# Two scattered rows per node, summed at the end, or one row per node to which the scatters add

## The chip, the cores and the metric

The kernel runs on one core of one Trainium2 chip. The metric is the time that the device takes for one launch, in microseconds (us). Before the change it is 1894.54 us, the median of three runs (1893.64 to 1895.57).

A core has five engines that work side by side, each on its own ordered list of instructions. TensorE (PE in the profile) does matrix products and has a separate step that loads weights (PEld). VectorE (DVE) and ScalarE (ACT) do elementwise work and sums. GpSimd (POOL) does some elementwise work and issues the indirect transfers: gathers and scatters of rows whose numbers are read from a list. SyncE (SP) issues most of the plain transfers. The transfers (DMA) move data between the large memory (HBM) and the on-chip memory (SBUF). Products are gathered in a small memory of their own, PSUM. An engine that needs the result of another, or of a transfer, waits for a semaphore; everything behind that instruction on the same engine waits too.

## The reference, cut to what matters

There are 3125 nodes with 256 features and 100,000 edges. The layer is

```python
xn = layernorm(x)
x  = x + gnn(xn, edge_attr_3, src, dst) + mixer(xn)     # mixer: 4 layers of linear attention and FFN
x  = x + ffn(layernorm(x))
```

The last line is a mixture of 16 experts, and the change touches only that part. For each node `y = layernorm(x)`:

```python
logits     = y @ gate_w + gate_b              # 16 numbers
vals, idx  = top_k(logits, 2)                 # the node's two experts
w          = softmax(vals)                    # two gates
e_k        = relu(y @ w1[idx_k] + b1[idx_k]) @ w2[idx_k] + b2[idx_k]    # 256 -> 512 -> 256
z          = y + w_0 * e_0 + w_1 * e_1
ffn(y)     = layernorm(z) * gamma + beta
```

So two experts' outputs of each node have to be added, with `y`, before the last normalisation. A sum over the 256 features of `z` cannot start before both are there.

## The kernel before, in words

**Tiling.** The nodes lie as 125 partitions by 25 tiles (`TP` = 125, `NT` = 25): partition p holds nodes 25p to 25p+24. `xm`, the running result, stays in SBUF for the whole kernel. The edge part and the first three mixer layers take the first 1600 us or so, and the change does not touch them.

**Dispatch, inside the last mixer layer.** The last mixer layer runs over seven blocks of nodes, the ranges in `BLOCKS`. Behind each block follow `stage_yn`, which normalises the block and stores *half* of `y` to the table `ynodes` in HBM; `stage_logits`, which picks the two experts and gates; and `stage_ranks`, which gives each (node, expert) pair a slot: expert e owns the slots that follow e * `CAP`. For each pair a record of three words (node, row of `outs` to write, gate) is scattered to the table `slots` in HBM. `prepare`, called in block 0 of that layer, clears what must be clear beforehand: it sets the rows of `ynodes` that are not yet written to zero, and fills `slots` with records of unused slots, each of which names a row of its own behind the real ones. Its stores go on SP's queue, where `slots`, and after them the loads `xr` and `xnT` of the next blocks, stand behind.

**The table `outs`.** It has two rows per node and one row per slot: `K * N + NSL` rows of 256 numbers. The first choice of node n goes to row n, the second to row N + n, and unused slots write rows that nobody reads. So no two slots write the same row.

**Expert tiles.** A tile is one expert and 128 or 256 of its slots, in blocks of 128. For each tile SP loads `ids` (128 records a block) and `ew` (the expert's weights, 1154 KB); POOL gathers the nodes of each block from `ynodes` into `yg` (L140); PE transposes them (`stage_t`), multiplies with `w1` (`stage_e1`), and with `w2` (`stage_e2`). DVE adds `b2` and then forms gate * expert + half of y in `o` (L209), and POOL scatters the 128 rows of `o` to `outs` (L211). The two halves of y that a node's two slots bring make the whole y.

- Four full tiles of two blocks are worked inside the first phase, behind the last mixer block ("early" tiles). They use memory that is free by then: `mem_h`, that is `hNT`, holds their weights, `mem_q`, that is `qT`, their `yg`, `hs` and `o`.
- The other tiles are worked by `run_tiles` in the second phase: 16 of one block and 17 of two blocks, mostly by turns. It loads `ids` six tiles ahead (nine buffers), weights and nodes three ahead (four buffers of `ew`, six of `yg`); `o` has three buffers. On PE and ACT the order is that of the program text. The line `stage_e2(xs[i - 1], 1)`, with tile i-1's last scatter, stands behind the load of the nodes of tile i+3, and so POOL's queue alternates between gathers and scatters.
- Two branches (`tc.If`) follow for more tiles than that; with these inputs nothing is in them to do.

**What orders the scatters.** The planner that places semaphores would make two writes to one table wait for each other. Here each scatter is put in a group, "combine", whose members are declared free of each other:

```python
tc.declare_no_dep(i.ins, group="combine", reason="every slot has a row of its own")
tc.add_to_no_dep_group("combine", i.ins)
```

So a scatter waits only for its `o`. What waits for a scatter's landing is the next user of its buffers (`ids`, `o`), and the output stage.

**Output stage.** It goes in ten parts of the 25 tiles (`ends`). SP loads both rows of each node into `ogs` (125 x 2 x 25 x 256), in 40 transfers, since `by_parts` cuts each into 112 and 13 partitions. PE adds the two rows by two products with the identity into PSUM (`sum_ps`, L1429). DVE takes mean and variance from there (`stats`: L91, L92), for the last tile of the larger parts ACT does (`act_stats`); ACT takes the root, DVE the reciprocal (L1452), ACT normalises from PSUM into `ogs` (L1456), DVE multiplies by `gamma` (L1461) and adds `xm` (L1462), which has `beta` in it already, and the part is stored.

**Memory.** `ogs`, `gamma` and an unused tile called `room` lie at the start of the second phase's memory; the weights' buffers `ew` and the tiles' working buffers follow. Nothing there is used before the first phase has left the addresses below it, and the planner adds the waits for that.

Of the kernel before, what the change touches and what calls it, by code (L numbers as in the profile page):

```python
# [16 lines left out]
N = 3125  # L17
# [24 lines left out]
K = 2  # L42
# [23 lines left out]
def gps_layer(ctx: ExitStack, tc: tile.TileContext, a, out):  # L66
# [10 lines left out]
    def by_tile(rows):  # L77

        return rows.rearrange("(p t) d -> p t d", t=NT)
# [20 lines left out]
    ynodes = tables.tile([N, D], F32, name="ynodes")  # L100
    slots = tables.tile([NSL, 3], I32, name="slots")

    outs = tables.tile([K * N + NSL, D], F32, name="outs")

    rs_v = consts.tile([TP, NT], F32, name="rs_v")
    rs_u = consts.tile([TP, NT], F32, name="rs_u")
# [24 lines left out]
    def registers(to, ap, most):  # L131
        to.extend(nc.values_load_multi_w_load_instructions(
            ap, engines=SP, min_val=0, max_val=most,
            skip_runtime_bounds_check_because="its parts are cut off above")[1])

    def expert_stages(new, mm_tile, fm_tile):
        def load_nodes(x):
# [54 lines left out]
        def stage_e2(x, part):  # L192
            n, ids = x["n"], x["ids"]
            if part == 0:
                x["e2"] = mm_tile("e2_ps").rearrange("p (j d) -> p j d", d=D)
                x["o"] = new("o")
            ps, o = x["e2"], x["o"]
            fs = range(NEF)
            if n == 1:
                fs = range(part * NEF // 2, (part + 1) * NEF // 2)  # L200
            j = part if n == 2 else 0

            for f in fs:
                nc.tensor.matmul(ps[:, j, :], x["hs"][:, f, j * P:(j + 1) * P], x["w2"][:, f, :],
                                 start=(f == 0), stop=(f == NEF - 1))
            if fs[-1] < NEF - 1:
                return
            nc.vector.tensor_add(o[:, j, :], ps[:, j, :], x["b2"])
            nc.vector.scalar_tensor_tensor(o[:, j, :], o[:, j, :], ids.bitcast(F32)[:, j, 2:3],  # L209
                                           x["yg"][:, j, :], op0=ALU.mult, op1=ALU.add)  # L210
            i = nc.gpsimd.indirect_dma_start(  # L211
                out=outs, out_offset=bass.IndirectOffsetOnAxis(ap=ids[:, j, 1:2], axis=0),
                in_=o[:, j, :], in_offset=None)
            tc.declare_no_dep(i.ins, group="combine", reason="every slot has a row of its own")
            tc.add_to_no_dep_group("combine", i.ins)

        return load_nodes, load_weights, stage_t, stage_e1, stage_ht, stage_e2

# [1 line left out]
    with ExitStack() as ph:  # L220
# [835 lines left out]

        def prepare():
            nc.gpsimd.memset(none, 0.0)
            for r in BLOCKS[-3:]:
                by_parts(nc.sync, by_tile(ynodes)[:, r[0]:r[-1] + 1, :], none[:, :len(r), :])  # L1060
            nc.gpsimd.memset(unused, 0)
            nc.gpsimd.iota(unused[:, :, 1], pattern=[[1, NSL // P]], base=K * N, channel_multiplier=NSL // P)
            nc.sync.dma_start(slots.rearrange("(p j) c -> p j c", p=P), unused)
            for k in range(K):
                nc.gpsimd.iota(rec[:, :, k, 0], pattern=[[1, NT]], base=0, channel_multiplier=NT)
                nc.gpsimd.iota(rec[:, :, k, 1], pattern=[[1, NT]], base=k * N, channel_multiplier=NT)
            nc.gpsimd.iota(eid, pattern=[[1, E]], base=0, channel_multiplier=0,
                           allow_small_or_imprecise_dtypes=True)
            nc.vector.memset(earlier, 1.0)
            nc.gpsimd.affine_select(out=earlier, in_=earlier, compare_op=ALU.is_gt, fill=0.0, base=0,  # L1070
                                    pattern=[[1, TP]], channel_multiplier=-1)
            nc.vector.memset(every, 1.0)
            nc.vector.tensor_scalar(run[:, 0, :], eid, float(CAP), None, op0=ALU.mult)
            nc.gpsimd.iota(tid, pattern=[[1, NFX]], base=0, channel_multiplier=0,
                           allow_small_or_imprecise_dtypes=True)
            nc.gpsimd.iota(spare, pattern=[[ST, NFX + NFE]], base=E * CAP, channel_multiplier=0,
                           allow_small_or_imprecise_dtypes=True)
            nc.vector.memset(one, 1.0)
            nc.vector.tensor_scalar(slot0, eid[:1], float(CAP), None, op0=ALU.mult)
# [243 lines left out]
    with ExitStack() as ph:  # L1323
# [6 lines left out]
        def mm_tile(name):  # L1330
            return psum.tile([P, 512], F32, tag="mm", name=name)

        ogs = big.tile([TP, K, NT, D], F32, name="ogs")
        gamma = big.tile([P, D], F32, name="gamma")

        big.tile([P, 2304], F32, name="room")
# [77 lines left out]
        ends = [1, 3, 5, 8, 11, 15, 19, 22, 24, NT]  # L1414
        parts = [range(i, j) for i, j in zip([0] + ends, ends)]
        for r in parts:
            for k in range(K):
                by_parts(nc.sync, ogs[:, k, r[0]:r[-1] + 1, :],
                         by_tile(outs[k * N:(k + 1) * N, :])[:, r[0]:r[-1] + 1, :])
        pss = {}  # L1420

        def sums(r):
            for q in groups(len(r), 2):
                t0, m = r[q[0]], len(q)
                pool, tag = ((psum, "mm"), (ps_f, "fm"))[q[0] // 2]
                ps = pool.tile([P, 512], F32, tag=tag, name="sum_ps")[:TP, :m * D].rearrange(
                    "p (i d) -> p i d", d=D)
                for k in range(K):
                    nc.tensor.matmul(ps, ident[:TP, :TP], ogs[:, k, t0:t0 + m, :],  # L1429
                                     start=(k == 0), stop=(k == K - 1))  # L1430
                for i in range(m):
                    pss[t0 + i] = ps[:, i, :]
                    if len(r) < 3 or t0 + i < r[-1]:
                        stats(tmp, ps[:, i, :], t0 + i)
                    else:
                        act_stats(ps[:, i, :], t0 + i)

        def act_stats(src, t):
            sq = tmp.tile([TP, D], F32, name="sq")
# [10 lines left out]
        def normalized(r, tt):  # L1450
            nr = tmp.tile([TP, 4], F32, name="nr")
            nc.vector.reciprocal(rstd[:, tt], rs_v[:, tt])  # L1452
            nc.vector.scalar_tensor_tensor(nr[:, :len(r)], mv[:, tt, 0], -1.0, rstd[:, tt], op0=ALU.mult,  # L1453
                                           op1=ALU.mult)
            for i, t in enumerate(r):
                nc.scalar.activation(ogs[:, 0, t, :], pss[t], AF.Identity, scale=rstd[:, t:t + 1],  # L1456
                                     bias=nr[:, i:i + 1])

        def stored(r, tt):
            ys = ogs[:, 0, tt, :]  # L1460
            nc.vector.tensor_mul(ys, ys, gamma[:TP, None, :].to_broadcast([TP, len(r), D]))  # L1461
            nc.vector.tensor_add(ys, ys, xm[:, tt, :])  # L1462

            by_parts(nc.gpsimd if r[0] < 15 else nc.sync, ov[:, tt, :], ys)

        with tc.manual_schedule(engines={mybir.EngineType.PE, mybir.EngineType.Activation, mybir.EngineType.DVE}):
            last = None
            for r in parts:
                sums(r)
                tt = scales(r)  # L1470
                if last:
                    stored(*last)
                normalized(r, tt)
                last = r, tt
            stored(*last)
# [61 lines left out]
```

## Time and profile before

| what | where from | value |
|---|---|---|
| time of a launch | median of three runs | 1894.54 us |
| profiled execution | one run with the profiler | 2133.78 us, span 2132.1 us, mean granted clock 0.934 |
| last mixer layer's first part, 1600 to 1680 us | table by stage | PE busy 80.00 of 80, clock 1.00, DMA 0.20 |
| rest of it with the early tiles, 1680 to 1880 us | table by stage | PE busy 190.92 of 200, clock 0.98, DMA 0.26 |
| expert tiles, 1890 to 2048 us | table by stage | PE busy 156.64 of 158, clock 1.00, DMA 0.79 |
| last tiles and branches, 2048 to 2086 us | table by stage | PE busy 27.32 of 38, clock 0.90, DMA 0.29 |
| output stage, 2086 to 2132 us | table by stage | PE busy 25.20, DVE 29.74, ACT 21.09 of 46, clock 0.83, DMA 0.68 |

The profile records one execution, and this one took longer than the runs that make up the median; a duration from the profile belongs to the profiled execution. The page gives for each engine its busy time, its share of the span and the number of its instructions. A table by stage has for each stretch of time (from:to, in us) its length, then busy time and number of instructions of each engine, the mean clock that was granted to PE, the mean share of the DMA engines that was busy, and what they moved in GB/s. A row of an engine's order of time has the start and the duration in us, the engine, the line, what was written and read, and in brackets how long the engine had been idle before and what ended that ("issue" is time in which it waited for nothing that the profile shows). SPq is the queue of transfers that SP issues: its rows show how long SP stood at the issue.

### The profile page before, as it was taken

Reading aid. Unit: us, or ns where it says so; the run is one execution under the profiler, and the core shown is the slowest. Engines: PE = TensorE matmul, PEld = TensorE weight load, DVE = VectorE, ACT = ScalarE, POOL = GpSimd, SP = SyncE. Lnnn points to the kernel's source line nnn. Section 1 sums busy time; section 2 is a strip of 40 time slices with the busy share of each in tenths; the row PEclk is TensorE's granted clock in tenths of the full one; section 3 lists DMA queues with packets and bytes.
Section 4 is the critical chain, followed back from the end, with each engine's and each line's share of the span. In section 5 each row is a group of like instructions: output and inputs, shape, how many; then the busy total and the mean of one; then the engine's idle time right before and its main releaser. Section 6 shows DMA issues by size and latency. Waiting matters only on the chain. (4 is left out here: it accounts for less than half of the span.)

```text
span 2132.1 us, 28655 instructions
## 1 busy us (share of the span) xinstructions
PE 1909.3 (90%) x8973; PEld 1262.4 (59%) x8973; DVE 1162.0 (54%) x3717; ACT 755.9 (35%) x1384; POOL 1107.4 (52%) x1407
## 2 busy tenths in 40 slices
PE   8997997998888988899988889899989999899994
PEld 6764553555554554555654445555676777778772
DVE  8664544645564545555565456555565566533335
ACT  4532433334423434344423334344422223222223
POOL 0027665675626666576636666676403334655441
PEclk9998998998998999889999889999999999999997
DMA  7122222232322222232332222232222100478755
GB/s 201 54 71 81 86 85 76 81 89 75 106 82 83 79 80 84 75 87 85 109 92 79 75 78 85 84 88 81 80 81 75 42 18 16 139 252 291 267 189 182
DMA packets 95904, 216.64 MB, mean 102 GB/s; under 512 B 26922, under 2 KB 53928, under 8 KB 91008
## 3 DMA queue, kind: packets, MB, share of 16 engines
q0 software_dynamic: 45488, 120.08, 19.6%
q1 hardware_dynamic: 50256, 94.62, 14.1%
q8 instruction: 77, 1.26, 0.3%
q14 instruction: 83, 0.68, 0.1%
HBM read 192.20 MB, written 22.35 MB: 101 GB/s over the span
## 5 line engine op out<-in xcount | busy, mean ns | idle before, releaser
L347 POOL DMA_INDIRECT gat<-proj,src_i x784 | 759.0, 968 | 231.2 <-issue 186.4
L750 PE MATMUL f_ps<-h2T,ww 128*128 128x500 f32 (+2 forms) x896 | 376.2, 569 | 24.0 <-ACT h2T L458 13.6
L760 PE MATMUL f_ps<-ww,gT 128*125 128x256 f32 x1600 | 379.1, 392 | 11.6 <-issue 7.4
L760 PEld LDWEIGHTS f_ps<-ww,gT 128*125 128x125 f32 x1600 | 301.4, 192 | 91.5 <-issue 33.0
L397 ACT ACTIVATE gat<-gat 128x512 f32<-128x512 f32 x392 | 238.4, 630 | 294.7 <-DVE gat L396 220.1
L396 DVE TENSOR_TENSOR gat<-gat,pw 128x512 f32<-128x512 f32 x392 | 251.7, 677 | 161.0 <-PE pw L391 79.3
L750 PEld LDWEIGHTS f_ps<-h2T,ww 128*128 128x128 f32 x896 | 172.3, 199 | 206.4 <-issue 140.0
L752 ACT ACTIVATE gT<-f_ps,ffb 128x500 f32<-128x500 f32 (+2 forms) x224 | 135.5, 631 | 142.0 <-PE f_ps L750 117.4
L377 PE MATMUL pq<-gat,hot 128*32 128x256 f32 x1568 | 152.4, 403 | 28.8 <-ACT gat L397 17.7
L391 PE MATMUL pw<-w1w,ea 8*128 8x512 f32 x784 | 143.0, 667 | 24.6 <-DVE rs_u L115 9.3
L380 ACT COPY osb<-pq 128x256 f32<-128x256 f32 x98 | 36.4, 372 | 310.6 <-remote 109.8
L369 DVE TENSOR_TENSOR hNT<-hNT,win_ps 128x64 f32 x392 | 84.4, 215 | 109.6 <-PE win_ps L366 38.1
L399 DVE TENSOR_TENSOR hot<-slot,drel 128x256 f32<-128x256 f32 x98 | 46.4, 475 | 153.8 <-remote 47.4
L765 DVE TENSOR_TENSOR xm<-xm,f_ps 125x512 f32<-125x512 f32 (+1 forms) x52 | 34.6, 666 | 151.7 <-PE f_ps L760 87.4
L587 PE MATMUL q_ps<-wwq,hT 128*125 128x256 f32 x400 | 108.0, 426 | 9.6 <-DVE gat L396 4.3
L644 PE MATMUL m_ps<-xh,ek 125*128 125x257 f32 x400 | 104.7, 413 | 10.6 <-issue 5.0
L1229 POOL DMA_INDIRECT slots<-rec,at x50 | 59.4, 1188 | 104.9 <-DVE rs_u L115 63.8
L703 PE MATMUL y_ps<-mo,qT 128*125 128x256 f32 x400 | 103.4, 410 | 10.1 <-issue 3.7
L377 PEld LDWEIGHTS pq<-gat,hot 128*32 128x32 f32 x1568 | 52.4, 111 | 97.2 <-issue 40.7
L587 PEld LDWEIGHTS q_ps<-wwq,hT 128*125 128x125 f32 x400 | 83.3, 214 | 36.0 <-DVE gat L396 6.6
L703 PEld LDWEIGHTS y_ps<-mo,qT 128*125 128x125 f32 x400 | 78.8, 203 | 35.1 <-issue 11.2
L644 PEld LDWEIGHTS m_ps<-xh,ek 125*128 125x128 f32 x400 | 81.1, 207 | 29.3 <-issue 7.9
(278 smaller groups left out, 2693.6 us busy)
## 6 DMA issues: line engine op xcount, KB each, us to landing
ew<-ffn_w SPq DMA_DIRECT2D x33, 1154.0 KB
gat<-proj,src_i POOLq DMA_INDIRECT x784
ww<-mix_W SPq DMA_DIRECT2D x8, 1024.0 KB
ea<-ea_g SPq DMA_DIRECT2D x98, 64.0 KB
hNT<-ffn_w SPq DMA_DIRECT2D x4, 1154.0 KB
xnT_d<-stage SPq DMA_DIRECT2D x5, 500.0 KB
xnT<-xnT_d SPq DMA_DIRECT2D x5, 500.0 KB
xr<-x SPq DMA_DIRECT2D x5, 448.0 KB
```

The costliest lines, as they stand in the source:

```text
L347: nc.gpsimd.indirect_dma_start(out=gats[-1][:, (j // SC) % 2, j % SC, :], out_offset=None, in_=proj, in_offset=bass.IndirectOffsetOnAxis(a ...
L369: nc.vector.tensor_add(win, win, pt[:, :, s * W:(s + 1) * W])
L377: nc.tensor.matmul(pq[s * W:(s + 1) * W, :], hot[:, s * SC + i, :], gats[s // 2][:, s % 2, i, :], start=(i == 0), stop=(i == SC - 1))
L391: nc.tensor.matmul(pws[s], ea[s * W:s * W + SC * 4, :], w1w[s * W:s * W + SC * 4, :], start=True, stop=True)
L396: nc.vector.tensor_add(msg, msg, pws[s])
L397: nc.scalar.activation(msg, msg, AF.Relu)
L587: nc.tensor.matmul(ps[:, i, :], st["hT", b][:, c, cols(o + i)], wt["Wq"][:, c, :], start=(c == 0), stop=(c == KC - 1))
L644: nc.tensor.matmul(ps, st["ek", b][:, i, c * P:(c + 1) * P], xh1s[b % 2][:, i, :], start=(i == 0), stop=(i == n - 1))
L703: nc.tensor.matmul(ps[:, i, :], qT[:, c, cols(t0 + i)], mo[:, c, :], start=(c == 0), stop=(c == KC - 1))
L750: nc.tensor.matmul(ps, wt["W1"][:, c, f * P:(f + 1) * P], st["h2T", b][:, c, :m], start=(c == 0), stop=(c == KC - 1))
L752: nc.scalar.activation(gT[:, f, :m], ps, AF.Gelu, bias=ffb[:, l, f:f + 1])
L760: nc.tensor.matmul(ps[:, i, :], st["gT", b][:, f, cols(o + i)], wt["W2"][:, f, :], start=(f == 0), stop=(f == NF - 1))
```

## The change

`outs` keeps one row per node, `N + NSL` rows in all. It is set to zero in `prepare`. Both slots of a node carry the same row number, and the scatter adds to the row that is there, where it wrote before. Since two tiles may now hold the same node, all scatters of one tile form a group that is free of each other (a tile has one expert, and a node chooses an expert once), but scatters of different tiles are not in one group any more. The output stage loads one row per node; its products with the identity are gone, the statistics and the normalisation read `ogs` in SBUF. `ogs` has half its size, and the memory behind it moves down by 25.6 KB a partition.

```diff
-    outs = tables.tile([K * N + NSL, D], F32, name="outs")
+    outs = tables.tile([N + NSL, D], F32, name="outs")
...
+    combined = []
...
         def stage_e2(x, part):
...
+            if j == 0:
+                x["combine"] = f"combine{len(combined)}"
+                combined.append(x)
             i = nc.gpsimd.indirect_dma_start(
                 out=outs, out_offset=bass.IndirectOffsetOnAxis(ap=ids[:, j, 1:2], axis=0),
-                in_=o[:, j, :], in_offset=None)
-            tc.declare_no_dep(i.ins, group="combine", reason="every slot has a row of its own")
-            tc.add_to_no_dep_group("combine", i.ins)
+                in_=o[:, j, :], in_offset=None, compute_op=ALU.add)
+            tc.declare_no_dep(i.ins, group=x["combine"], reason="a tile's slots have a node each")
+            tc.add_to_no_dep_group(x["combine"], i.ins)
...
         def prepare():
             nc.gpsimd.memset(none, 0.0)
+            for r in BLOCKS:
+                by_parts(nc.sync, by_tile(outs[:N])[:, r[0]:r[-1] + 1, :], none[:, :len(r), :])
             for r in BLOCKS[-3:]:
                 by_parts(nc.sync, by_tile(ynodes)[:, r[0]:r[-1] + 1, :], none[:, :len(r), :])
             nc.gpsimd.memset(unused, 0)
-            nc.gpsimd.iota(unused[:, :, 1], pattern=[[1, NSL // P]], base=K * N, channel_multiplier=NSL // P)
+            nc.gpsimd.iota(unused[:, :, 1], pattern=[[1, NSL // P]], base=N, channel_multiplier=NSL // P)
...
-                nc.gpsimd.iota(rec[:, :, k, 1], pattern=[[1, NT]], base=k * N, channel_multiplier=NT)
+                nc.gpsimd.iota(rec[:, :, k, 1], pattern=[[1, NT]], base=0, channel_multiplier=NT)
...
-        ogs = big.tile([TP, K, NT, D], F32, name="ogs")
+        ogs = big.tile([TP, NT, D], F32, name="ogs")
...
         for r in parts:
-            for k in range(K):
-                by_parts(nc.sync, ogs[:, k, r[0]:r[-1] + 1, :],
-                         by_tile(outs[k * N:(k + 1) * N, :])[:, r[0]:r[-1] + 1, :])
-        pss = {}
-
-        def sums(r):
...
-                for k in range(K):
-                    nc.tensor.matmul(ps, ident[:TP, :TP], ogs[:, k, t0:t0 + m, :],
-                                     start=(k == 0), stop=(k == K - 1))
...
+            by_parts(nc.sync, ogs[:, r[0]:r[-1] + 1, :], by_tile(outs[:N])[:, r[0]:r[-1] + 1, :])
+
+        def moments(r):
+            for t in r:
+                if len(r) < 3 or t < r[-1]:
+                    stats(tmp, ogs[:, t, :], t)
+                else:
+                    act_stats(ogs[:, t, :], t)
...
-                nc.scalar.activation(ogs[:, 0, t, :], pss[t], AF.Identity, scale=rstd[:, t:t + 1],
+                nc.scalar.activation(ogs[:, t, :], ogs[:, t, :], AF.Identity, scale=rstd[:, t:t + 1],
                                      bias=nr[:, i:i + 1])
...
-            ys = ogs[:, 0, tt, :]
+            ys = ogs[:, tt, :]
...
-                sums(r)
+                moments(r)
```

More of the change, by code (lines that the diff above doesn't have):

```diff
@@ L1416, in gps_layer @@
         for r in parts:
-            for k in range(K):
-                by_parts(nc.sync, ogs[:, k, r[0]:r[-1] + 1, :],
-                         by_tile(outs[k * N:(k + 1) * N, :])[:, r[0]:r[-1] + 1, :])
-        pss = {}
-        def sums(r):
[L1423 to L1427, printed above, removed]
-                for k in range(K):
-                    nc.tensor.matmul(ps, ident[:TP, :TP], ogs[:, k, t0:t0 + m, :],
-                                     start=(k == 0), stop=(k == K - 1))
[L1431 to L1436, printed above, removed]
+            by_parts(nc.sync, ogs[:, r[0]:r[-1] + 1, :], by_tile(outs[:N])[:, r[0]:r[-1] + 1, :])
[5 more added lines that the diff above has]
+                    act_stats(ogs[:, t, :], t)
         def act_stats(src, t):
```

## The prediction

> **What bounds the kernel now.** I read the page first, then the stages by time, then the queues around the scatters. The first two lines below are the page's; the other two are rows of the table by stage (length, busy us and instructions of PE, PE's loads, DVE, ACT and POOL, granted clock, DMA share, GB/s). The change touches only what begins near 1600 us, so the whole-span shares say little.
>
> ```profile
> span 2132.1 us, 28655 instructions
> PE 1909.3 (90%) x8973; PEld 1262.4 (59%) x8973; DVE 1162.0 (54%) x3717; ACT 755.9 (35%) x1384; POOL 1107.4 (52%) x1407
> ...
> 1900.00:1950.00 50.00, 50.00 (x234) 40.28 (x233) 18.93 (x43) 14.40 (x31) 25.63 (x27) 1.00 0.79 277
> 1950.00:2000.00 50.00, 49.34 (x237) 40.28 (x236) 19.14 (x44) 14.02 (x32) 25.50 (x26) 1.00 0.80 269
> ```
>
> In the expert stage PE is the bound at full clock, and the DMA engines are 0.8 busy with weights: almost no room beside either. Next, POOL's order of time in that stage (start, us, line, what; in brackets the idle time and who ended it).
>
> ```profile
> 1952.40 0.99 POOL L211 DMA_INDIRECT outs<-o,ids  x1 [1.17 <-DVE o L209]
> 1955.00 0.99 POOL L211 DMA_INDIRECT outs<-o,ids  x1 [1.61 <-DVE o L209]
> 1956.30 0.99 POOL L140 DMA_INDIRECT yg<-ynodes,ids  x1 [0.30 <-issue]
> 1957.60 0.97 POOL L140 DMA_INDIRECT yg<-ynodes,ids  x1 [0.30 <-issue]
> 1960.40 0.99 POOL L211 DMA_INDIRECT outs<-o,ids  x1 [1.84 <-DVE o L209]
> 1961.70 0.98 POOL L140 DMA_INDIRECT yg<-ynodes,ids  x1 [0.30 <-issue]
> 1963.84 0.98 POOL L211 DMA_INDIRECT outs<-o,ids  x1 [1.17 <-DVE o L209]
> 1966.45 0.98 POOL L211 DMA_INDIRECT outs<-o,ids  x1 [1.62 <-DVE o L209]
> ```
>
> The two-block tile's scatters (F0, F1) are at 1952.40 and 1955.00, then come two gathers, the one-block tile's scatter (S) at 1960.40, a gather, and F0 and F1 of the next at 1963.84 and 1966.45. A pair of tiles takes 1966.45 - 1955.00 = 11.45 us, and every scatter waits for DVE, that is for its data, never for a DMA.
>
> How long a scatter needs to land is not a row of its own, but two waits show it. SP may refill a tile's `ids` only when that tile's scatters have landed, and it stands there; and the memset of `eps` on DVE stood behind the last early scatter.
>
> ```profile
> 1909.21 0.99 POOL L211 DMA_INDIRECT outs<-o,ids  x1 [1.61 <-DVE o L209]
> 1943.55 1.00 POOL L211 DMA_INDIRECT outs<-o,ids  x1 [1.61 <-DVE o L209]
> ...
> 1909.13 7.91 SPq L1350 DMA_DIRECT2D ids<-slots  x2
> 1944.03 6.16 SPq L1350 DMA_DIRECT2D ids<-slots  x2
> ...
> 1880.51 0.98 POOL L211 DMA_INDIRECT outs<-qT,ids  x1 [0.63 <-issue]
> 1886.18 0.06 DVE L1413 MEMSET eps<- 125x1 f32 x1 [5.95 <-DMA outs<-qT,ids]
> ```
>
> SP's second refill starts 0.33 us before the row ends: 1916.71 - 1909.21 = 7.50 us and 1949.86 - 1943.55 = 6.31 us from the scatter's start to its landing. The same reading of the seven pairs between 1897 and 1973 us gives 5.55 to 7.61, mean 6.4. The early one: 1886.18 - 1880.51 = 5.67. So a plain scatter lands in about 6.4 us beside the weight stream.
>
> At the end, the chain that ended last goes through the second If and then the output stage.
>
> ```profile
> 2077.04 8.94 DMA outs<-o,ids
> ...
> 2093.83 6.15 DMA ogs<-outs
> ...
> 2100.36 9.17 DMA ogs<-outs
> 2109.58 2.85 PE sum_ps L1429 x6
> ```
>
> **The change, part by part.** The sum is made against the profiled execution, 2133.8 us (span 2132.1), which is 239 us above the median of 1894.5; the touched stages ran at clock 1.00 and are bound by PE, DMA latency and DVE, so I carry the difference over unscaled (scaled by 0.89 it would be 5 us less).
>
> *Zeroing.* 14 more SP transfers, 3.2 MB, go ahead of the zeroing of `ynodes` at 1604.67. At SP's 0.4 us per transfer 5.6 us of issue, at some 230 GB/s 14 us of data, so `slots`, `xr` and `xnT` land about 14 us later. POOL already waits 4.76 us for `xr` at 1619.52; it would go on near 1633, its next own work is at 1637.90, and in the built program DVE's use of that sum stands behind the `yb` rows (1636 to 1638) where it stood before them. `xnT`, issued at 1616.46, is needed by PE at 1648.74. Price 0; without that cover up to 14 us. Scatters to slots begin only at 1676.
>
> *The order of the scatters.* In the built program the first scatter of each tile waits for the landing of the previous tile's last one: S for the preceding F1, F0 for S. F1 does not wait for F0. A pair then takes at least L (S) + L (F1) + 1.3 us (F1 is issued that much after F0: 0.99 and 0.30 of issue) + 2 x 0.3 us from a landing to the start (the rows' 0.30). The three gathers of a pair, 3.9 us, fit under the two landings. Nothing else is queued on POOL. With L = 6.4 for both: 14.7 us against 11.45, +3.25 per pair. From 1891.22 (first S) to 2048.22 (last F1 beside weights) there are 157 / 11.45 = 13.7 pairs: **+44.5 us**. Who waits: `o` has three buffers, so DVE's write of tile i stands until tile i-3 has landed, relus and PE behind it. The gathers for tile i+4 come behind the scatter of tile i; they have two pairs, 28 us, where gather, transposes and both products take about 18, so they add nothing.
>
> *The accumulation.* Each scatter reads its 128 old rows too. No row of before shows one. Two rules stand beside the landing row. The Trainium skill, DMA: Bandwidth & Descriptors, Anatomy of one DMA, puts such a transfer at about 2.0 us + bytes / 436e3: an estimate of 2.3 us for 128 KB, with which a pair needs 6.5 us and the chain costs nothing; the row says 5.6 to 7.6 beside the weights, and the row decides there. Against the change speaks Collectives: The Full Stack, The bandwidth ceiling: an addition in a DMA needs two source reads, hence twice the read descriptors on the same ring. If landing were read traffic alone that doubles L to 12.8: 27.5 us a pair, +220 us; no run here shows how much of L is that. I take L = 6.4, the row: a lighter weight stream (9 us of transfers in 14.7, not in 11.45) takes off some of what the second read adds. Ends: 4.8, where the chain just fits into 11.45, and 9, half of the doubling: 19.9 us a pair, +116.
>
> *The quiet end.* After the last weights five tiles remain, 2048.22 to 2077.04 = 28.8 us. With L about 3.5 (between 2.3 and 5.67) the chain needs 5 x 3.8 + 3 x 1.3 = 23, and PE is ahead of it: **-5** (0 to -6).
>
> *The moved buffers.* `ogs` halves (25.6 KB less a partition), and all that is allocated behind it moves down. In before, the first weights of the stage lay clear of the early tiles and were loaded at 1841.06. In the changed program they lie over `hNT`, which holds the early tiles' weights, and SP waits for PE, DVE and the landing of all early scatters. The last of them starts at 1880.51; with no weights in flight L is 3.5, so 1884.0; +0.4; a weight load takes 4.8 us (issued at 1890.45, released ACT at 1895.26): 1889.2 instead of 1880.83 for the first product. The next weights follow 4 us later, 0.5 more than PE's step: **+9** (7.5 to 11). SP's `ids` and POOL's first gathers wait too, under the same 9 us.
>
> *Output stage.* 40 loads become 20, 6.4 MB become 3.2; 18 groups of PE sums go. DVE is 29.74 us busy of 38.5 between 2090.5 and 2129, and its work stays (statistics from SBUF cost what those from PSUM do: 0.42 and 0.43 us). Of its idle time only 1.59 + 0.54 + 0.85 + 0.54 = 3.5 us were waits for the sums, and the first part comes about 2.2 us sooner: **-6**. If DVE ran without any gap, -10; if the waits turn to ACT, -3. The 8.94 us after the last scatter are engines going through the two Ifs, and stay.
>
> Sum: 44.5 - 5 + 9 - 6 = +42.5 us, 1937.
>
> **Rivals.**
> (a) The waits are covered: L below (11.45 - 1.9) / 2 = 4.8 us. For it: the 2.3 us of the page, and lighter traffic; against it: no landing read above is below 5.5. Then +9 - 6 = 1897.5; with the output stage at -10 and the early landing at 2.3 (+7.5), 1892: not slower. It decides where L falls under 4.8 and the output gains more than the late weights lose.
> (b) The accumulation is the bound: the second read makes L 9 or more, for the reason of the rule above; +116 - 5 + 9 - 6 = 2008, and 2110 at 12.8. Against it: much of 6.4 is queueing behind weight packets, which does not double.
> (c) The zeroing isn't hidden, PE stands for `xnT` or `xr`: 14 us more, 1951. Against it: 32 us of slack for `xnT`.
> That the sums stay exact needs each wait; no wait is optional, so the chain cannot be absent.
>
> **How the numbers follow.** Main case 0.65 (1912 to 1985, L from 5.4 to 8), (a) 0.14, (b) 0.16, (c) 0.05. Range 1896 to 2006: it leaves out the lower half of (a) and most of (b)'s upper end. This kernel's measurement can tell about 0.2%, 3.8 us, from no change. Of (a) half is within that and some 0.05 below it: faster 0.06, same 0.07, slower 0.87.
>
> **What would show it.** POOL's scatters ended by DMA `outs`, not by DVE `o`; 14 to 16 us a pair; PE below 0.85 busy in the stage; first weights after the early scatters, PE idle some 9 us near 1881; no stall near 1620 to 1650; output stage near 40 us instead of 46. The prediction fails if an accumulating scatter lands much faster or slower than 6.4 us, or if PE finds other work ahead.

## The result, and the profile after

The changed kernel takes 1973.88 us (median of four runs, 1965.94 to 1975.52) against 1894.21 us for the kernel before (the three runs shown ahead and one more): a ratio of 1.0406, with a 95% interval of 1.0385 to 1.0427, or 79.7 us more. The forecast was 1937 us, 42.5 us more, with a range of 1896 to 2006. Direction and range held; the loss is almost twice the central number. Of the experiments below, the first four ran beside a kernel before of 1893.61 us (mean granted clock 0.98) and the others on chips that granted less (0.93; the kernel before takes 2151.85 and 2133.08 us there), so "over before" means over the runs of the kernel before on the same chip.

First the page of the changed kernel, then two rows of its table by stage (columns as in the prediction).

```profile
span 1972.8 us, 28502 instructions
PE 1788.5 (91%) x8913; PEld 1215.8 (62%) x8913; DVE 1159.7 (59%) x3717; ACT 757.3 (38%) x1384; POOL 1146.4 (58%) x1407
...
1750.00:1800.00 50.00, 38.74 (x162) 29.66 (x162) 12.18 (x28) 9.78 (x21) 23.51 (x18) 0.90 0.66 189
1800.00:1850.00 50.00, 39.64 (x161) 29.57 (x160) 13.16 (x30) 9.40 (x20) 23.33 (x18) 0.90 0.66 189
```

In the expert stage PE is busy 39 of 50 us where it was 49 to 50, and does some 161 products in that time instead of 235. The DMA engines are less busy too (0.66 against 0.79): nothing is saturated, the stage waits. POOL's order of time shows for what, with DVE's write of the data and SP's queue of the same microseconds below it:

```profile
1798.13 1.62 POOL L217 DMA_INDIRECT outs<-o,ids  x1 [0.36 <-issue]
1800.06 0.98 POOL L142 DMA_INDIRECT yg<-ynodes,ids  x1 [0.30 <-PE e_ps L206]
1807.84 1.59 POOL L217 DMA_INDIRECT outs<-o,ids  x1 [6.80 <-DMA outs<-o,ids]
1809.73 1.59 POOL L217 DMA_INDIRECT outs<-o,ids  x1 [0.30 <-issue]
1811.62 1.02 POOL L142 DMA_INDIRECT yg<-ynodes,ids  x1 [0.30 <-PE e_ps L206]
1812.95 0.98 POOL L142 DMA_INDIRECT yg<-ynodes,ids  x1 [0.30 <-issue]
1814.41 1.62 POOL L217 DMA_INDIRECT outs<-o,ids  x1 [0.48 <-issue]
...
1800.82 0.48 DVE L211 SCALAR_TENSOR_TENSOR o<-o,ids,yg 128x256 f32<-128x256 f32 x1
...
1790.96 6.87 SPq L1358 DMA_DIRECT2D ids<-slots  x2
1797.94 0.97 SPq L149 DMA_DIRECT2D ew<-ffn_w  x2
1807.09 7.06 SPq L1358 DMA_DIRECT2D ids<-slots  x2
1814.25 0.96 SPq L149 DMA_DIRECT2D ew<-ffn_w  x2
```

S (one-block tile) is at 1798.13, F0 and F1 (two-block tile) at 1807.84 and 1809.73, the next S at 1814.41. F0 had its data (DVE wrote its `o` until 1801.30), and POOL stood idle for 6.80 us before it, until S had landed. The three steps are 9.71 + 1.89 + 4.68 = 16.28 us; the mean of the ten pairs from 1699.29 to 1864.49 is 16.5 us. An adding scatter also holds POOL for 1.6 us where a plain one held it for 0.99.

SP shows why S is slow and F1 is not. It stands at a refill of `ids` until F1 has landed (1797.4; the row ends with the second refill, at 1797.83), and then issues the two weight loads that had queued behind it, 2.3 MB from 1797.94 on. S goes out 0.2 us after the first of them and lands behind both (1807.07; they land at 1803.37 and 1806.90); by the next F1 they are through. The trace's record of when each transfer raised its semaphore for the last time gives, as medians of eleven pairs, 9.07 us for S and 3.82 us for F1.

The late weights are also what PE stands for. Its longest waits in the stage (total us, times, longest) are, after (1672 to 1894 us) and, last line, before (1891 to 2048 us):

```profile
PE e_ps L169 <- DMA ew<-ffn_w: 35.6, 10, 5.6
PE e_ps L206 <- DVE o L210: 4.2, 2, 3.7
...
PE e_ps L167 <- DMA ew<-ffn_w: 1.2, 2, 0.7
```

Then the first weights (the `eps` row stands, as before, for the last early scatter), and the end (the first row is the first product of the kernel before):

```profile
1880.83 1.98 PE L167 MATMUL e_ps<-ew,ygT 128*128 128x512 f32 x4 [0.60 <-issue]
...
1646.60 1.56 POOL L217 DMA_INDIRECT outs<-qT,ids  x1 [0.30 <-issue]
1650.69 2.32 SPq L149 DMA_DIRECT2D ew<-ffn_w  x3
1650.76 0.06 DVE L1421 MEMSET eps<- 125x1 f32 x1 [5.01 <-DMA outs<-qT,ids]
1651.40 1.02 POOL L142 DMA_INDIRECT yg<-ynodes,ids  x1 [3.25 <-issue]
1658.96 0.66 PE L159 MATMUL ygT_ps<-ident,yg 128*128 128x128 f32 x2 [14.19 <-issue]
1660.22 1.22 PE L169 MATMUL e_ps<-ew,ygT 128*128 128x512 f32 x1 [0.60 <-ACT ygT L161]
...
1918.18 3.82 DMA outs<-o,ids
...
1922.72 8.55 DMA outs<-o,ids
```

The first product comes 13.6 us after the last early scatter's start; before it was 0.3. The weights go out as soon as that scatter has landed, and the first of them land at 1656.61. But the gather issued at 1651.40, with three weight loads and four `ids` issued around it, lands only at 1658.55, and PE starts on it at 1658.96. In the chain of waits, tail scatters follow each other by their landings (3.82 us without weights in flight).

Where the 79.7 us are, from the starts of the scatters in the two profiled executions (mean granted clock 0.934 before, 0.960 after):

| stretch | before, start to start | after | difference | forecast |
|---|---|---|---|---|
| first to last early scatter | 1853.9 to 1880.5: 26.6 | 1617.0 to 1646.6: 29.6 | +3.0 | 0 |
| to the first later scatter (S) | to 1891.2: 10.7 | to 1672.1: 25.5 | +14.8 | +9 |
| to the last F1 beside weights | to 2048.2: 157.0 | to 1894.2: 222.1 | +65.1 | +44.5 |
| to the last scatter | to 2077.0: 28.8 | to 1922.7: 28.5 | -0.3 | -5 |
| to the end of the span | to 2132.1: 55.1 | to 1972.8: 50.1 | -5.0 | -6 |
| sum | 278.2 | 355.8 | +77.6 | +42.5 |

In a second profiled execution of the changed kernel these stretches take 350.2 us instead of 355.8, so a few us of such a difference lie between executions.

The zeroing shows nowhere: around its stores PE is busy throughout, although the DMA engines are 0.92 busy for 10 us.

```profile
1370.00:1380.00 10.00, 10.00 (x32) 5.91 (x31) 4.49 (x12) 3.40 (x5) 9.27 (x14) 1.00 0.71 228
1380.00:1390.00 10.00, 10.00 (x48) 8.99 (x47) 5.20 (x24) 1.20 (x2) 1.72 (x1) 1.00 0.92 285
1390.00:1400.00 10.00, 10.00 (x49) 8.33 (x48) 3.56 (x9) 1.01 (x2) 2.35 (x1) 1.00 0.35 100
```

### The profile page after: what moved, and what is told of

The parts are those of the page before. It is cut to its first block, busy times and chain, and to the rows that moved or that the text cites. A ratio compares the mean times of both kernels' runs of the same rounds, so it can differ in the third digit from the quotient of the medians.

```text
span 1972.8 us, 28502 instructions
## 1 busy us (share of the span) xinstructions
PE 1788.5 (91%) x8913; PEld 1215.8 (62%) x8913; DVE 1159.7 (59%) x3717; ACT 757.3 (38%) x1384; POOL 1146.4 (58%) x1407
## 3 DMA queue, kind: packets, MB, share of 16 engines
q0 software_dynamic: 51056, 120.08, 23.2%
HBM read 189.00 MB, written 25.55 MB: 109 GB/s over the span
## 5 line engine op out<-in xcount | busy, mean ns | idle before, releaser
L756 PE MATMUL f_ps<-h2T,ww 128*128 128x500 f32 (+2 forms) x896 | 361.2, 551 | 6.6 <-ACT h2T L464 5.9
L766 PE MATMUL f_ps<-ww,gT 128*125 128x256 f32 x1600 | 363.3, 382 | 0.0
L217 POOL DMA_INDIRECT outs<-o,ids x50 | 80.6, 1613 | 118.0 <-DMA outs<-o,ids 48.3
L383 PE MATMUL pq<-gat,hot 128*32 128x256 f32 x1568 | 130.3, 388 | 11.3 <-ACT gat L403 10.7
L397 PE MATMUL pw<-w1w,ea 8*128 8x512 f32 x784 | 119.4, 639 | 0.6 <-ACT gT L758 0.3
L1237 POOL DMA_INDIRECT slots<-rec,at x50 | 59.5, 1190 | 100.9 <-DVE rs_u L115 63.7
L206 PE MATMUL e_ps<-ew,hs 128*128 128x256 f32 x400 | 102.7, 396 | 4.6 <-DVE o L210 4.5
L210 DVE TENSOR_TENSOR o<-e_ps,ew 128x256 f32<-128x256 f32 x50 | 21.2, 425 | 133.0 <-PE e_ps L206 112.4
L709 PE MATMUL y_ps<-mo,qT 128*125 128x256 f32 x400 | 94.6, 388 | 2.7 <-DVE mo L699 2.7
L593 PEld LDWEIGHTS q_ps<-wwq,hT 128*125 128x125 f32 x400 | 77.2, 198 | 28.7 <-DVE gat L402 8.6
L206 PEld LDWEIGHTS e_ps<-ew,hs 128*128 128x128 f32 x400 | 78.1, 202 | 25.4 <-issue 9.6
L569 PE MATMUL k_ps<-hT,wwk 128*128 128x500 f32 (+2 forms) x224 | 92.3, 556 | 1.6 <-DVE hT L466 0.8
```

The costliest lines, as they stand in the source:

```text
L383: nc.tensor.matmul(pq[s * W:(s + 1) * W, :], hot[:, s * SC + i, :], gats[s // 2][:, s % 2, i, :], start=(i == 0), stop=(i == SC - 1))
L397: nc.tensor.matmul(pws[s], ea[s * W:s * W + SC * 4, :], w1w[s * W:s * W + SC * 4, :], start=True, stop=True)
L593: nc.tensor.matmul(ps[:, i, :], st["hT", b][:, c, cols(o + i)], wt["Wq"][:, c, :], start=(c == 0), stop=(c == KC - 1))
L709: nc.tensor.matmul(ps[:, i, :], qT[:, c, cols(t0 + i)], mo[:, c, :], start=(c == 0), stop=(c == KC - 1))
L756: nc.tensor.matmul(ps, wt["W1"][:, c, f * P:(f + 1) * P], st["h2T", b][:, c, :m], start=(c == 0), stop=(c == KC - 1))
L766: nc.tensor.matmul(ps[:, i, :], st["gT", b][:, f, cols(o + i)], wt["W2"][:, f, :], start=(f == 0), stop=(f == NF - 1))
```

## The experiments

**The first four: order alone, addition alone, memory, and SP's queue.** Two theories stood against each other: A, the order costs, with a landing behind two weight loads as its longest term; B, the addition inside the transfer costs.

*The order alone*, in the kernel before:

```diff
+            if j == 0:
+                x["combine"] = f"combine{len(combined)}"
+                combined.append(x)
...
-            tc.declare_no_dep(i.ins, group="combine", reason="every slot has a row of its own")
-            tc.add_to_no_dep_group("combine", i.ins)
+            tc.declare_no_dep(i.ins, group=x["combine"], reason="a tile's slots have a node each")
+            tc.add_to_no_dep_group(x["combine"], i.ins)
```

> The kernel before with the order alone: each tile's scatters form a group, so the first scatter of a tile waits for the landing of the tile before, but they write plainly to two rows, and buffers, zeroing and output stage stay as before. Theory A (the order is the cost, and a landing behind two weight loads is its longest term): a pair of tiles takes 14 to 15 us instead of 11.45, since a plain scatter lands a little sooner than an adding one and takes 0.6 us less of POOL; 13.7 pairs give +35 to +48, 1930 to 1942 us. Theory B (the addition in the transfer is the cost, the order only shows it): under 1 us a pair, 1908 us at most.

Measured: 1904.46 us, 10.9 over before (ratio 1.0062, 1.0032 to 1.0092). The time is in B's range and far from A's. POOL's scatters:

```profile
1702.00 1.00 POOL L216 DMA_INDIRECT outs<-o,ids  x1 [0.30 <-issue]
1710.08 0.99 POOL L216 DMA_INDIRECT outs<-o,ids  x1 [5.81 <-DMA outs<-o,ids]
1711.38 1.00 POOL L216 DMA_INDIRECT outs<-o,ids  x1 [0.30 <-issue]
1715.25 0.99 POOL L216 DMA_INDIRECT outs<-o,ids  x1 [0.30 <-issue]
```

A pair takes 12.87 us (1677.10 to 1818.69, eleven pairs), 1.4 more than before where B had said under 1: plain scatters land in 6.92 us (S) and 2.44 us (F1), medians, not in the 12 us or more together that A had assumed. The order alone makes the stage 18.0 us longer (175.0 us), and the tail, where tiles follow each other by 2.4 us landings, 6.1 us shorter (22.7).

*The addition alone*, in the kernel before, with both rows zeroed:

```diff
+            for k in range(K):
+                for r in BLOCKS:
+                    by_parts(nc.sync, by_tile(outs[k * N:(k + 1) * N])[:, r[0]:r[-1] + 1, :], none[:, :len(r), :])
...
-                in_=o[:, j, :], in_offset=None)
+                in_=o[:, j, :], in_offset=None, compute_op=ALU.add)
```

> The kernel before with the addition alone: scatters add to two rows per node, both set to zero by 28 stores at the start of the last mixer layer, and no scatter waits for another. Theory A: POOL's six instructions a pair grow from 7.7 to 9.6 of 11.45 us, nothing waits, and the time is 1892 to 1902 us. Theory B: the second read doubles the landing to 12 us or more, buffers of ids and o come free late, and the time is 1935 us or more.

Measured: 1900.25 us, 6.6 over before (ratio 1.003, 1.002 to 1.0039), as A had it. The landings are long (8.70 us for F0, 7.50 for F1, 4.14 for S, medians), and no scatter waits for one; POOL's order of time:

```profile
1727.18 1.63 POOL L211 DMA_INDIRECT outs<-o,ids  x1 [1.22 <-DVE o L209]
...
1730.62 1.58 POOL L211 DMA_INDIRECT outs<-o,ids  x1 [0.52 <-DVE o L209]
1733.22 1.57 POOL L211 DMA_INDIRECT outs<-o,ids  x1 [1.02 <-DVE o L209]
```

The releasers are those of the kernel before, the scatters 0.6 us longer each. So 10.9 and 6.6 us alone, against 79.7 together: each theory explained one run and failed in the other. The theory that took their place is that order and addition multiply: a landing costs only what of it stands uncovered between two tiles. The order uses up the cover (12.87 against 11.45), and from there almost all that the addition lengthens counts, at every one of some 14 pairs.

*The old addresses*, in the changed kernel:

```diff
-        big.tile([P, 2304], F32, name="room")
+        big.tile([P, 2304 + NT * D], F32, name="room")
```

> The changed kernel with the unused tile 25.6 KB a partition larger, so that the weights' and tiles' buffers lie where they lay before. Theory A (the late first weights cost what the trace shows, 17.8 us from the first early scatter to the first later one): 12 to 18 us less, 1956 to 1962 us. Rival C (the tiles are then only ahead of the chain of scatters, which takes as long): within 5 us of the changed kernel, 1969 to 1979 us.

Measured: 1959.67 us, 66.1 over before, 14.2 less than the changed kernel, in A's range. The stretches say it less simply. From the last early to the first later scatter it is 8.2 us instead of 25.5, as expected. But the early tiles' scatters, now beside weight loads and in order, take 36.3 us instead of 29.6, and the stage 226.3 instead of 222.1; so the touched stretches are only 6.4 us shorter (349.4), and the rest lies ahead of the change, where executions differ anyway. By the stretches the result is nearer to C: most of what the early start gains, the chain of scatters takes back.

*More `ids` buffers*, in the changed kernel, so that SP doesn't stand:

```diff
-    bufs = dict(ids=lambda: tmp.tile([P, 2, 3], I32, name="ids", bufs=9),
+    bufs = dict(ids=lambda: tmp.tile([P, 2, 3], I32, name="ids", bufs=12),
```

> The changed kernel with twelve buffers of ids instead of nine, so that SP no longer stands at a refill until a scatter has landed and then issues two weight loads at once, just ahead of the one-block tile's scatter. Theory A: that scatter lands in 5 to 7 us instead of 9, a pair takes 13 to 14 us instead of 16.3, and the time is 1925 to 1950 us. Theory B (a landing beside weights is slow however they are issued): within 5 us of the changed kernel, 1969 to 1979 us.

Measured: 1952.8 us, 59.2 over before (48.3 to 68.5), 21 less than the changed kernel: between the two, by the touched stretches (342.9) 12.9 less. S lands in 5.82 us instead of 9.07, as A said. But F1 now takes 5.27 (medians; up to 8.9 in some pairs) instead of 3.82, and a pair still takes 15.6 us. S, F0, F1, the next S, and SP's queue:

```profile
1761.18 1.63 POOL L217 DMA_INDIRECT outs<-o,ids  x1 [0.39 <-DVE hs L182]
1767.68 1.58 POOL L217 DMA_INDIRECT outs<-o,ids  x1 [3.59 <-DMA outs<-o,ids]
1769.57 1.57 POOL L217 DMA_INDIRECT outs<-o,ids  x1 [0.30 <-issue]
1775.59 1.62 POOL L217 DMA_INDIRECT outs<-o,ids  x1 [1.84 <-issue]
...
1764.83 6.51 SPq L149 DMA_DIRECT2D ew<-ffn_w  x2
```

The two weight loads now go out 6 us apart (1764.83 and 1771.00) and land at 1772.63 and 1777.58, so F1 meets weights too. Only part of S's gain is left. SP stands for a refill of `ids` no longer (0.2 us in the stage instead of 155.0), but until DVE has read a weights' buffer for the last time (173.2). PE stands for DVE's `o` (28.9 us), and DVE for landings of scatters (60.8): with SP's stand gone, the chain of scatters reaches PE by `o`.

**Four that take one part out.** *Plain scatters in the changed kernel*:

```diff
-                in_=o[:, j, :], in_offset=None, compute_op=ALU.add)
+                in_=o[:, j, :], in_offset=None)
```

> The changed kernel with scatters that write instead of add, everything else as changed, the tile-by-tile order too; one row per node, so the second expert overwrites the first and the sum is left out. Theory A (order and addition multiply: the addition's longer landing costs only where the next scatter waits for it): a pair of tiles takes about 12.9 us as in the kernel with the order alone, and with the late first weights (+14) and the shorter output stage (-5) the time is 1905 to 1922 us. Theory B (the addition adds a fixed 6 us, as it does without the order, and the rest is memory placement): 1960 us or more.

Measured: 22.8 us over before (ratio 1.0111, 1.0066 to 1.0155). A's range was 11 to 28 over, B's 66 or more. POOL's order of time of this kernel:

```profile
2003.36 1.02 POOL L217 DMA_INDIRECT outs<-o,ids  x1 [0.30 <-DVE o L210]
2004.68 0.98 POOL L142 DMA_INDIRECT yg<-ynodes,ids  x1 [0.31 <-PE e_ps L177]
2011.38 1.00 POOL L217 DMA_INDIRECT outs<-o,ids  x1 [5.71 <-DMA outs<-o,ids]
2012.68 0.99 POOL L217 DMA_INDIRECT outs<-o,ids  x1 [0.30 <-issue]
2013.97 1.00 POOL L142 DMA_INDIRECT yg<-ynodes,ids  x1 [0.30 <-issue]
2015.27 0.97 POOL L142 DMA_INDIRECT yg<-ynodes,ids  x1 [0.30 <-issue]
2016.55 1.00 POOL L217 DMA_INDIRECT outs<-o,ids  x1 [0.30 <-issue]
```

S at 2003.36 and F0 and F1 at 2011.38 and 2012.68 give steps of 8.02 + 1.30 + 3.87 us; the last is no landing but POOL's own work, F1 and two gathers. Over eleven pairs the means are 7.53 + 1.30 + 4.20 = 13.03. The stage is 175.2 us long and the tail 22.3, with the order and the moved memory in place. With the addition they are 222.1 and 28.5. So of the 79.7 us some 53 (46.9 + 6.2; 50 with the second execution of the changed kernel, 218.8 and 29.2) come only when the addition stands inside the order.

*The zeroing alone*, in the kernel before:

```diff
+            for r in BLOCKS:
+                by_parts(nc.sync, by_tile(outs[:N])[:, r[0]:r[-1] + 1, :], none[:, :len(r), :])
```

> The kernel before with the 14 stores of zeros to the first row of each node ahead of the others in the last mixer layer, nothing else changed. As predicted, they are hidden: 1892 to 1897 us. If the last mixer layer stands for its loads behind them: up to 14 us more, 1900 to 1908 us.

Measured: 5.4 us under before (ratio 0.9978, 0.9956 to 1.0001). The loss of 14 us is excluded; that it costs nothing agrees with the PE rows above. A gain is not shown, the interval reaches no change.

*The output stage alone*, in the kernel before, with the second row left out:

```diff
-        ogs = big.tile([TP, K, NT, D], F32, name="ogs")
+        ogs = big.tile([TP, NT, D], F32, name="ogs")
...
-        big.tile([P, 2304], F32, name="room")
+        big.tile([P, 2304 + NT * D], F32, name="room")
...
-                sums(r)
+                moments(r)
```

> The kernel before with the output stage of the changed one, the memory behind it kept in place: it loads only the first row of each node, and the second expert's row is left out of the sum. As predicted: 4 to 7 us less, 1887 to 1890 us. If the stage is bound by DVE and ACT alone and the loads and sums were hidden: within 2 us, 1892 to 1896 us.

Measured: 1.6 us under before (ratio 0.9988, 0.9965 to 1.0011): the interval holds both numbers, and the run doesn't tell them apart. In its trace the last scatter lies 50.8 us before the end of the span, where it is 55.1 before, much as in the changed kernel (50.1): by the traces the gain is there, by the times it stays open.

*Half the weights*, in the changed kernel:

```diff
-            nc.sync.dma_start(ew, w.rearrange("o p n -> p (o n)"))
-            x.update(w1=ew[:, :KC * EF].rearrange("p (c n) -> p c n", c=KC),
+            nc.sync.dma_start(ew[:, KC * EF:], w.rearrange("o p n -> p (o n)")[:, KC * EF:])
+            x.update(w1=ew[:, KC * EF:2 * KC * EF].rearrange("p (c n) -> p c n", c=KC),
```

> The changed kernel with half of each expert's weights left out of the load (the first product uses the second's weights, and the result is not the layer's). Theory A (the one-block tile's scatter lands in 9 us because it is queued behind two weight loads): it lands in 5 to 7 us, a pair takes 12 to 14 us, and the time is 1915 to 1945 us. Theory B (the read and write of the addition make it 9): at most 6 us less than the changed kernel, 1966 us or more.

Measured: 35.8 us over before (ratio 1.0156, 1.0111 to 1.02); A's range was 21 to 51 over, B's 72 or more. POOL's order of time:

```profile
2035.78 1.62 POOL L217 DMA_INDIRECT outs<-o,ids  x1 [0.42 <-issue]
2042.57 1.59 POOL L217 DMA_INDIRECT outs<-o,ids  x1 [3.89 <-DMA outs<-o,ids]
```

S to F0 is 6.79 us instead of 9.71, and S lands in 6.21 us (median of eleven) instead of 9.07; a pair takes 13.7 us. Leaving out half of the weights takes 2.9 us off the landing. In the changed kernel S lands 5.3 us later than F1, which has no weights beside it: S's time is mostly time behind weights.

**Three on distance.** *Two tables by kind of tile*: the adding scatters and their order, but one-block tiles add to one table and two-block tiles to the other (both set to zero, 28 stores); output stage as before.

```diff
-    outs = tables.tile([N + NSL, D], F32, name="outs")
+    outs = [tables.tile([N + NSL, D], F32, name=f"outs{k}") for k in range(K)]
...
-                out=outs, out_offset=bass.IndirectOffsetOnAxis(ap=ids[:, j, 1:2], axis=0),
+                out=outs[x["n"] - 1], out_offset=bass.IndirectOffsetOnAxis(ap=ids[:, j, 1:2], axis=0),
```

> The changed kernel's adding scatters and their order by tiles, but in two tables: one-block tiles add to one, two-block tiles to the other, and output stage and memory are those of the kernel before. A scatter then waits only for the landing of the tile before last, and between them lies a whole pair. Theory A (what costs is that every landing stands between two neighbouring tiles): the two-block chain needs a landing of 8 to 9 us + 0.75 + 1.9 = 10.7 to 11.7 us a pair, about the 11.45 there are, and the time over the kernel before is 0 to 15 us. Theory D (adding and ordering cost the DMA engines or POOL more than they have, however they are chained): 40 us over or more.

Measured: 11.4 us over before (ratio 1.0055, 1.0032 to 1.0079), as A had it. The stage is 157.6 us long, and was 157.0 before the change. Two rows of its table by stage, and POOL's order of time:

```profile
1950.00:2000.00 50.00, 49.36 (x232) 39.96 (x231) 19.23 (x44) 13.35 (x29) 33.11 (x26) 1.00 0.94 268
2000.00:2050.00 50.00, 48.99 (x232) 39.61 (x230) 18.01 (x41) 14.31 (x31) 33.16 (x27) 1.00 0.95 275
...
2004.36 1.62 POOL L217 DMA_INDIRECT outs<-o,ids  x1 [1.21 <-DVE o L211]
2006.29 0.99 POOL L142 DMA_INDIRECT yg<-ynodes,ids  x1 [0.30 <-issue]
2008.53 1.58 POOL L217 DMA_INDIRECT outs<-o,ids  x1 [1.26 <-DVE o L211]
2011.14 1.57 POOL L217 DMA_INDIRECT outs<-o,ids  x1 [1.02 <-DVE o L211]
```

PE is full again, the DMA engines are 0.94 busy, POOL 33 of 50, and the scatters wait for their data. The same additions are ordered too, each behind the tile before last; that a landing has a whole pair of tiles to pass in, instead of standing between two neighbours, takes 64.5 of the 65.1 us away. All touched stretches are 283.3 us long, 5.1 more than before; the early tiles, all of two blocks and so still one chain, are 6.9 of it (33.5 against 26.6; the additions alone, without any order, took 31.2 there, so the chain is not shown to be the whole reason), and the other stretches give 1.8 back. What of the 11.4 us is beyond that is not seen in them.

*Both easings in the changed kernel* (the larger unused tile and twelve `ids` buffers), *and the changed kernel again*:

> The changed kernel with the larger unused tile and the twelve buffers of ids together. If the two gains (14 and 21 us) lie in different stretches, as theory A has it, they add up to 30 to 38 us less than the changed kernel, 42 to 50 us over the kernel before. If both free the same chain of scatters, the gain is that of one, 15 to 22 us less, 58 to 65 us over.

> The changed kernel again, beside the two others on the same chip: 72 to 86 us over the kernel before, also where the kernel before itself is slow, since the touched stages ran at full clock.

Measured: the changed kernel is 67.3 us over before (ratio 1.0328, 1.0252 to 1.0405), that is 54 to 86 us, and less in the middle than the 72 to 86 expected; its touched stretches take 350.2 us, 72.0 more than before. Both easings give 59.5 over before (1.0218 to 1.0377), 332.4 us in these stretches. By the medians the gain is 7.8 us with an interval as wide as the question; by the traces it is 17.8 us. The expected 30 to 38 is in neither; it was summed from medians, of which a part lies ahead of the change. By the touched stretches the easings gained 6.4 and 12.9 us alone, 19.3 in sum, and 17.8 together: they add up there, as far as single executions tell that differ by 5.6 us for the same kernel. Neither version comes near the kernel before.

## Why the prediction was right or wrong

**Right: the mechanism and most of its signs.** Scatters released by `outs` instead of `o`, PE at 0.78 of the stage's middle, PE idle near the first weights (14.2 us, not 9), no stall at the zeroing, an output stage of about 41 us: these are in the trace. A pair takes 16.3 to 16.5 us, just above the 14 to 16. The choice to carry the differences over unscaled held (77.6 us in the profiled executions, 79.7 in the medians), though its reason, a clock of 1.00, is true of the expert stage alone; the tail had 0.90 and the output stage 0.83.

**Right chain, wrong path to PE.** "DVE's write of tile i stands until tile i-3 has landed, relus and PE behind it" is not what the changed kernel shows. PE stands 35.6 us for weights and 4.2 for DVE's `o`: the landing of F1 holds SP's refill of `ids`, and that holds the weights. This link was not in the prediction, and it is also what sends two weight loads out beside every S. With twelve `ids` buffers the path by `o` is there as forecast.

**The order of the scatters: mis-sized, 44.5 forecast, 65.1 measured.** The formula was L(S) + L(F1) + 1.3 + 2 x 0.3. The landings were right in their sum only, 12.8 forecast, 9.07 + 3.82 = 12.9 measured: all seven landings that were read are those of an F1, and neither S nor F1 now lands in anything like 6.4. The prediction itself had called that a sign of failure; that 9.07 and 3.82 have the forecast sum is luck. What failed in the sum were the small terms. F1 follows F0 by 1.89 us, not 1.3, since the adding instruction holds POOL for 1.6 us. And from a landing to the start of the scatter that waits for it pass 0.7 to 0.8 us (F1 at 1894.23 + 3.9, next S at 1898.85), not 0.3, which is the gap between two instructions of POOL where nothing is awaited; with plain scatters the wait costs the same 0.77 us. These are 0.6 + 2 x 0.45 = 1.5 us a pair, and 13.7 x 1.5 = 20.6 us: about the whole miss in this stretch, on average (the first two pairs take 13.6 us each, the ten that follow 16.5).

**The addition: right by luck, two errors that cancelled.** The step said that a lighter weight stream takes off what the second read adds. Shown apart: with order and plain scatters the landings are 6.9 and 2.4 us, 9.3 in sum and not 12.8, because F1 now lands with no weights beside it (2.44 us, as in the tail); the addition brings 2.1 us for S and 1.4 for F1, back to 12.9. So most of what the forecast put under "order" is the addition's: the order alone made the stage 18.0 us longer, the addition inside it 46.9 more. The two bounds of that step can be judged too. The estimate of 2.3 us from the Trainium skill's Anatomy of one DMA (DMA: Bandwidth & Descriptors) is near what a plain scatter takes without other traffic, 2.4 us. The two source reads of an addition come from the skill's Collectives: The Full Stack, The bandwidth ceiling, which speaks of the reduction in a collective; the prediction carried them over as a doubling of the landing. Measured is a factor of 1.6 without other traffic (3.8 against 2.4) and 1.3 beside weights (9.07 against 6.92). That the second read is the reason for either is not shown by any run. Rival (b) named the larger part of the cause, the addition, and set it too high.

**The quiet end: the step failed, -5 forecast, -0.3 measured.** L was taken as 3.5 us with 0.3 to the start; an adding scatter takes 3.8 and 0.75. (The sum as it stands gives 5 x 3.8 + 3 x 1.3 = 22.9, so -5.9 rather than -5.) Five steps of 4.6 and three of 1.9 make 28.7 us, as much as the scatters' data took before. With plain scatters the forecast would have held (22.3 and 22.7 us in the two kernels that have them).

**The moved buffers: +9 forecast, +14.8 measured.** The wait for the last early landing was right (1650.69 - 1646.60 = 4.1 us, 3.9 forecast). The step that failed is "SP's `ids` and POOL's first gathers wait too, under the same 9 us": the first gather started beside three weight loads and took 7.6 us to reach PE, so the nodes, not the weights, were last (1658.55 against 1656.61). The 3.0 us in the early tiles were not in the sum; when the changed kernel ran again they were 0.2 (26.8 us), so they are not shown to come from the change.

**Zeroing and output stage** came as forecast, 0 and -5.0 for -6, the second by the traces alone. In the range of the main case, L from 5.4 to 8 gives 1910 to 1981 us by the prediction's own formula, not 1912 to 1985; nothing hangs on it.

## What to carry to other kernels

Before a wait is put between neighbours, compare the landing of a transfer with the work between them, in the traffic that will then be there: here 11.45 us of work covered a plain landing chain almost (11 us lost), and what the addition put on top counted at every pair of tiles. Ask also what else waits for that landing: here a refill of `ids` did, and with it the weights. An operation that is free where nobody waits for it (adding scatters alone, 7 us) is not free behind such a wait; price changes together, not one by one. If an order is needed, give it more distance: two tables used by turns took the whole loss out of the stage.

## What the runs showed of the hardware

- A scatter of 128 rows of 1 KB holds POOL for 0.99 us when it writes and 1.58 us when it adds (medians, alike in all kernels). Its landing without other traffic takes 2.4 us and 3.8 us.
- From the landing of a scatter to the start of the scatter that stands for it pass 0.72 to 0.77 us, with plain and with adding scatters.
- Additions at the old pace (two tables) keep the DMA engines 0.94 to 0.95 busy, where plain scatters kept them 0.79 to 0.80 busy, at much the same 268 to 277 GB/s.
- The record of the DMA queues shows 5568 packets more in the software queue (45488 to 51056), exactly 96 for each of the 58 scatters, and no more bytes (120.08 MB in both). Every kernel here with adding scatters has the second number, every one with plain scatters the first.
- The bytes read from HBM fell from 192.20 to 189.00 MB, by the 3.2 MB that the output stage no longer loads; the old rows that the additions take in, 58 x 128 KB, do not appear in that count: with the addition alone, both rows loaded as before, it is 192.20 MB too.
